# A two-layer kernel whose instruction order is worked out by another model of time

## The chip, the cores and the metric

One core of a Trainium2 chip runs the whole program. A core has five engines with an instruction stream each, which meet only at semaphores: TensorE (PE in the profile, with its weight loads as PEld), VectorE (DVE), ScalarE (ACT), GpSimd (POOL) and SyncE (SP, which here only starts transfers). The metric is the device time of one execution in microseconds. The span of a profile runs from the first to the last instruction of the execution that the profiler recorded.

## The reference, cut to what matters

The input `x` is 4 batches of 512 tokens with 256 features, all in float32. Two layers follow each other.

```
xn = layernorm(x)
x  = x + linear_attention(xn) + gene_ffn(xn)          # layer 0
xn = layernorm(x)
x  = x + gated_mixer(xn) + moe(xn)                    # layer 1
```

- `linear_attention`: q, k, v projections, elu(.)+1 of q and k, the running sum of k times v along the tokens, times q, output projection.
- `gene_ffn`: logits of 512 genes per token, the 32 largest by `top_k`, a softmax over them, their gene vectors, and then tanh of one projection times another.
- `gated_mixer`: q, k, v, running sums of exp(k) v and exp(k) along the tokens, their quotient gated by sigmoid(q), then a SwiGLU block with a hidden width of 1024: `x + u * silu(g) @ w_out.T`.
- `moe`: 16 experts with an inner width of 176, each token goes to its two best, and one shared expert of width 352 sees every token.

## The kernel before, in words

**Stages.** Layer 0 of a batch `b` is `front(b)` (L229: layer norm, transposes, projections, running sum, gene logits) and `back(b, i0, nt)` (L299: for each tile of 128 tokens the top 32 by four rounds of MAX8 and MATCH_REPLACE8 on DVE (L311, L312), then `express` (L321), and at last `out` (L346), the output projection, whose result L352 adds to `xs`). Layer 1 up to the SwiGLU block is `mix(b, i0, nt)` (L366). It takes statistics of `xs` (L203 to L211: DVE, a square root on ACT at L209, DVE), forms `xn` on ACT (L216), transposes it (L224), projects (L389), exponentiates (L415, L416), transposes `qk` and `vs` (L224 again), runs the scans `sums` (L426), two reciprocals of 256 columns for each half of the features (L435), and writes `yT` (L437). It also works out the tokens' two experts (`chosen`, `cwall`). Batch 0's `mix` runs in two halves of 256 tokens, the other batches' in one piece.

**Dense chunks.** The shared expert and the SwiGLU block are one generator, `dense` (L573). It has 8 halves of 256 tokens and 11 chunks of hidden columns in each: three of the shared expert, which need only `xn1T` of their tokens, and eight of the SwiGLU block, which need `yT`. A chunk is 4 matmuls into `gu` (L583; a float32 matmul is two passes in the profile), a nonlinearity into `hid`, and 2 matmuls into `acc` (L606), two chunks behind. The nonlinearity has two forms: while the list `calm` is empty, ACT copies `gu` out and POOL makes three products and sums (L594 to L597); once `calm` holds something, DVE does it in two instructions out of PSUM (L590, L591). Both start with a tanh on ACT (L587). After a half's last chunk L617 adds `acc` to `xs` on DVE.

**Experts.** `route` (L465) counts the tokens of each expert by two matmuls into `pr` (L491, L492) and turns them into row numbers (`slot`, L538). `scatter` (L546) writes the tokens' `xn` to the DRAM array `xrows`, sorted by expert, in 32 indirect transfers that POOL issues (L549). `experts` (L804) goes over 47 tiles of 128 rows in 24 pairs: fetch (`xg`, L741), transposes (L733), up (L770), down (L791), and a store to `yrows` (L802). At the end 32 indirect gathers on POOL (L836) fetch each token's two results as `ys`, and L847 adds them on DVE.

**What sets the order.** The generators are interleaved by hand with `together`, which takes steps from its streams in given proportions; `d(n)` stands for n chunks. That is the order in which instructions are recorded; 66 chunks are recorded before the experts and 22 beside the gathers. The tile framework's scheduler then makes each engine's own order out of the recorded list, by what is ready in its model of time, and gives out semaphores and buffers. `paced` (L92) makes a transfer wait for the last `acc` matmul recorded before it. Each engine runs its instructions strictly in the scheduler's order.

Buffers that matter: PSUM holds 3 `gu` and 1 `acc`, and there are 4 `hid`. `ones` (L107) is the constant row that the scans use, `both` (L593) the copy of `gu` for POOL; its pool `w2` is closed with `mixing` at L703.

Of the kernel before, what the change touches and what calls it, by code (L numbers as in the profile page):

```python
# [11 lines left out]
F32 = mybir.dt.float32  # L12
# [4 lines left out]
P = 128  # L17
B, L, D = 4, 512, 256
NT = L // P
# [11 lines left out]
HB = 2 * P  # L31
# [6 lines left out]
def run_all(steps):  # L38
    for _ in steps:
        pass  # L40


def together(*streams):

    live = [[iter(steps), n, 0] for steps, n in streams]
    while live:
        s = min(live, key=lambda s: s[2] / s[1])
        s[2] += 1
        if next(s[0], live) is live:
            live.remove(s)  # L50
# [3 lines left out]
def tile_two_layers(  # L54
# [21 lines left out]
    out: bass.AP,  # L76
):
    nc = tc.nc
    V, S, G, T = nc.vector, nc.scalar, nc.gpsimd, nc.tensor

    const = ctx.enter_context(tc.tile_pool(name="const", bufs=1))
# [22 lines left out]

    ident = const.tile([P, P], F32, name="ident")
    make_identity(nc, ident)
    ones = const.tile([P, L], F32, name="ones")  # L107
    G.memset(ones, 1.0)

    load_x(0)  # L110
    wqkv = wp.tile([P, NH, 3 * D], F32, name="wqkv")
# [67 lines left out]
    wd = ctx.enter_context(tc.tile_pool(name="wd", bufs=2))  # L179
# [4 lines left out]
    wk = mixing.enter_context(tc.tile_pool(name="wk", bufs=1))  # L184
    w2 = mixing.enter_context(tc.tile_pool(name="w2", bufs=2))
# [3 lines left out]
    def bank():  # L189
        return ps_m.tile([P, L], F32, name="pm")  # L190


    carry = wk.tile([P, 6], F32, name="carry")

# [351 lines left out]
    def scatter():  # L546
        for k in range(2):
            for i in range(NTT):
                sc = G.indirect_dma_start(  # L549
                    out=xrows,  # L550
                    out_offset=bass.IndirectOffsetOnAxis(ap=slot[:, k, i : i + 1], axis=0),
                    in_=xn1[:, i // NT, i % NT],
                    in_offset=None,
                ).ins
                tc.declare_no_dep(sc, group="scatter", reason="no two tokens share a row")
                tc.add_to_no_dep_group("scatter", sc)
                paced(sc)
                yield
# [12 lines left out]
    calm = []  # L571

    def dense():  # L573
# [5 lines left out]
        def up(ins, spare, gw, g0, uw, u0, m, which, dw, dc):  # L579
            gu = ps_d.tile([P, 2, HB], F32, name="gu")  # L580
            for k, (w, at) in enumerate(((gw, g0), (uw, u0))):
                for h in range(NH):
                    T.matmul(  # L583
                        gu[0:m, k], w[:, h, at : at + m], ins[which][:, h], start=(h == 0), stop=(h == NH - 1)
                    )
            th = wd.tile([P, HB], F32, name="th", bufs=2)
            S.activation(th[0:m], gu[0:m, 0], AF.Tanh, scale=0.5)  # L587
            hid = wd.tile([P, HB], F32, name="hid", bufs=4)
            if spare:
                V.scalar_tensor_tensor(th[0:m], th[0:m], 1.0, gu[0:m, 0], ALU.add, ALU.mult)  # L590
                V.tensor_tensor(hid[0:m], gu[0:m, 1], th[0:m], ALU.mult)  # L591
            else:
                both = w2.tile([P, 2, HB], F32, name="both")  # L593
                S.copy(both[0:m], gu[0:m])  # L594
                G.tensor_tensor(hid[0:m], both[0:m, 0], both[0:m, 1], ALU.mult)  # L595
                G.tensor_tensor(th[0:m], th[0:m], hid[0:m], ALU.mult)
                G.tensor_tensor(hid[0:m], hid[0:m], th[0:m], ALU.add)  # L597
            return hid
# [36 lines left out]
    dd = dense()  # L635

    def d(n):
        return islice(dd, n), n
# [29 lines left out]
    m2 = mix(2, 0, NT)  # L668
    next(m2)
    run_all(islice(dd, 2))  # L670
    together((m2, 9), (back(3, 0, NT), 12), d(9))
    first.close()

    weights = ctx.enter_context(ExitStack())
# [7 lines left out]
    def load_experts():  # L682
        wdv = w_down.rearrange("(e i) d -> i e d", i=NI)
        for e in range(0, NE, 4):
            es = slice(e, e + 4)
            for h in range(NH):
                paced(
                    nc.sync.dma_start(
                        wev[:, es, h * 2 * NI : (h + 1) * 2 * NI],
                        w_gate_up[es, h * P : (h + 1) * P, :].rearrange("e p j -> p e j"),  # L690
                    ).ins
                )
                yield
            paced(nc.sync.dma_start(wev[:, es, EW - 2 * D : EW - D], wdv[0:P, es]).ins)
            yield
            paced(nc.sync.dma_start(wev[0 : NI - P, es, EW - D : EW], wdv[P:NI, es]).ins)
            yield

    m3 = mix(3, 0, NT)
    next(m3)  # L700
    run_all(islice(dd, 2))
    together((m3, 9), d(5), (load_experts(), 17))
    mixing.close()  # L703
    routing = ctx.enter_context(ExitStack())
    calm.append(True)
    together((route(), 8), d(5))
    routing.close()
    together((scatter(), 33), d(15))

    run_all(islice(dd, 6))  # L710

    wx = ctx.enter_context(tc.tile_pool(name="wx", bufs=2))
    hbs = []
# [114 lines left out]
    back = ctx.enter_context(tc.tile_pool(name="back", bufs=1, side="right"))  # L828
# [77 lines left out]
```

## Time and profile before

| | us |
|---|---|
| runs | 599.85, 598.52, 599.7; median 599.7 |
| profiled execution | 600.71 |
| its span, first to last instruction | 599.0 |
| PE busy | 544.6 (91%) |
| weight loads busy | 390.5 (65%) |
| DVE busy | 342.2 (57%) |
| ACT busy | 265.9 (44%) |
| POOL busy | 236.2 (39%) |
| DMA queues of SP, and of POOL | 38.53 MB, 8.39 MB |

The busy times of different engines overlap. A stage is bound by the engine that is full in it, or by a chain of waits that goes from engine to engine; which of the two it is can be seen only stage by stage. An instruction's line is that of `kernel.py`; `x8` means that eight of a kind are put together. A wait in brackets is the idle time of the engine just before the instruction, with what ended it. The passes of PE are pipelined: one of 256 columns is listed with 384 ns, while the next one follows after 216 ns.

### The profile page before, as it was taken

To read this page: it belongs to the slowest core of one execution; us is meant where nothing else is said; L and a number is where in the kernel's file an instruction comes from. 1 tells how busy PE (TensorE), PEld (TensorE's weight loads), DVE (VectorE), ACT (ScalarE), POOL (GpSimd) and SP (SyncE) were. 2 spreads that over 40 slices of the span, in tenths; PEclk is the share of its full clock that TensorE was granted. 3 is DMA by queue.
4 is the path that set the end of the run, shared out by engine and by line. 5 is a ranking of instruction groups with operands and counts; after the bars stand their busy time and mean duration, and the time that the engine had idled before them with its cause. 6 is when DMAs were issued, how large, how long until landed. Compare 5 with 4: busy or idle time off the path is not lost.

```text
span 599.0 us, 7343 instructions
## 1 busy us (share of the span) xinstructions
PE 544.6 (91%) x2360; PEld 390.5 (65%) x2360; DVE 342.2 (57%) x890; ACT 265.9 (44%) x568; POOL 236.2 (39%) x298
## 2 busy tenths in 40 slices
PE   3949979899999989999899499699999999999897
PEld 1424457655676555756676388587777777788786
DVE  2899998289683949934842982232222222225553
ACT  3667865955467572668178011113333333321111
POOL 1332058386747172666782027650000000006651
PEclk9998979999999999999999989799999999999989
DMA  5992000000000000000069202223233333114441
GB/s 165 393 382 95 1 1 1 1 1 2 0 1 1 0 2 1 2 0 1 0 183 320 77 6 100 88 89 105 89 106 106 107 106 96 54 63 125 130 122 45
DMA packets 38453, 47.38 MB, mean 79 GB/s; under 512 B 4016, under 2 KB 34960, under 8 KB 38160
## 3 DMA queue, kind: packets, MB, share of 16 engines
q1 hardware_dynamic: 35344, 38.53, 19.8%
q0 software_dynamic: 3072, 8.39, 4.6%
q8 instruction: 19, 0.31, 0.2%
q14 instruction: 18, 0.15, 0.1%
HBM read 28.30 MB, written 18.61 MB: 78 GB/s over the span
## 4 chain that ended last, share of the span: by engine, by line
PE 56%; DVE 25%; ACT 7%; POOL 4%; issue 3%; another core or an unknown queue 2%; DMA 1%; SPq 0%; DVEq 0%; POOLq 0%; ACTq 0%
PE gu L583 16%; PE pu L770 9%; PE acc L606 8%; PE py L791 7%; PE pm L389 5%; DVE rep L312 5%; DVE top L311 4%; PE pt L733 3%; DVE sums L435 3%; PE pm L224 2%; DVE sums L426 2%; PE pm L283 2%; PE pm L334 1%; DVE bs L203 1%
## 5 line engine op out<-in xcount | busy, mean ns | idle before, releaser
L583 PE MATMUL gu<-yT,wugt 128*128 128x256 f32 x512 | 125.9, 384 | 0.0
L583 PEld LDWEIGHTS gu<-yT,wugt 128*128 128x128 f32 x512 | 96.8, 192 | 14.0 <-issue 1.4
L587 ACT ACTIVATE th<-gu 128x256 f32<-128x256 f32 (+1 forms) x88 | 33.5, 383 | 162.3 <-PE gu L583 97.6
L836 POOL DMA_INDIRECT ys<-yrows,slot x32 | 30.7, 961 | 153.4 <-PE acc L606 143.1
L606 PE MATMUL acc<-wot,hid 128*128 128x256 f32 x256 | 69.5, 390 | 13.3 <-DVE hid L591 13.3
L770 PE MATMUL pu<-wex,xgT 128*128 x188 | 63.8, 461 | 0.8 <-ACT xgT L747 0.8
L606 PEld LDWEIGHTS acc<-wot,hid 128*128 128x128 f32 x256 | 48.2, 194 | 21.3 <-DVE hid L591 14.1
L583 PE MATMUL gu<-xn1T,sgu 128*128 128x256 f32 (+1 forms) x192 | 51.1, 404 | 0.1
L590 DVE SCALAR_TENSOR_TENSOR th<-th,gu 128x256 f32<-128x256 f32 (+1 forms) x48 | 20.0, 417 | 53.5 <-ACT th L587 39.4
L779 DVE TENSOR_TENSOR hb<-pu,hb 128x176 f32<-128x176 f32 x47 | 16.1, 342 | 51.0 <-ACT hb L778 51.0
L389 PE MATMUL pm<-w,xn1T 128*128 128x512 f32 (+1 forms) x128 | 44.1, 494 | 0.5 <-ACT xn1T L377 0.5
L791 PE MATMUL py<-wex,hgT 128*128 x188 | 44.5, 379 | 0.0
L583 PEld LDWEIGHTS gu<-xn1T,sgu 128*128 128x128 f32 (+1 forms) x192 | 36.6, 196 | 9.8 <-issue 2.6
L595 POOL TENSOR_TENSOR hid<-both 128x256 f32<-128x256 f32 (+1 forms) x40 | 29.7, 743 | 33.5 <-ACT both L594 33.4
L791 PEld LDWEIGHTS py<-wex,hgT 128*128 128x128 f32 x188 | 35.6, 190 | 8.6 <-issue 0.2
L549 POOL DMA_INDIRECT xrows<-xn,slot x32 | 30.9, 966 | 24.9 <-DVE th L590 10.9
L770 PEld LDWEIGHTS pu<-wex,xgT 128*128 128x128 f32 x188 | 32.0, 190 | 11.0 <-ACT xgT L747 1.0
L389 PEld LDWEIGHTS pm<-w,xn1T 128*128 128x128 f32 x128 | 24.0, 190 | 21.6 <-issue 16.5
L783 DVE COPY hgT<-pt 128x512 f32<-128x512 f32 (+1 forms) x24 | 16.3, 680 | 34.2 <-PE pt L733 34.2
L283 PE MATMUL pm<-wct,xnT 128*128 128x512 f32 x64 | 32.4, 640 | 1.1 <-ACT xnT L242 1.1
L311 DVE MAX8 top<-rep 128x8 f32<-128x512 f32 x48 | 32.7, 682 | 0.3
L312 DVE MATCH_REPLACE8 rep<-top,rep 128x512 f32<-128x512 f32 x48 | 32.3, 674 | 0.0
(170 smaller groups left out, 968.2 us busy)
## 6 DMA issues: line engine op xcount, KB each, us to landing
xrows<-zero SPq DMA_DIRECT2D x1, 6016.0 KB, 22.5
xg<-xrows SPq DMA_DIRECT2D x23, 256.0 KB, 2.7
yrows<-yg SPq DMA_DIRECT2D x23, 256.0 KB, 2.1
wex<-in_w_gate_up_dram SPq DMA_DIRECT2D x8, 704.0 KB, 9.9
xs<-in_x_dram SPq DMA_DIRECT2D x4, 512.0 KB
wugt<-in_wug_dram SPq DMA_DIRECT2D x1, 2048.0 KB
wex<-in_w_down_dram SPq DMA_DIRECT2D x4, 512.0 KB
out_dram<-xs SPq DMA_DIRECT2D x7, 256.0 KB, 2.4
```

Source lines behind the costliest of these rows:

```text
L283: T.matmul(pl, xnT[:, h, i * P : (i + 1) * P], wct[:, h], start=(h == 0), stop=(h == NH - 1))
L311: V.max(tp[:, 8 * r : 8 * r + 8], src)
L312: V.match_replace(rep, tp[:, 8 * r : 8 * r + 8], src, TAKEN)
L389: T.matmul(o[:, 0:n], xnT[:, h, i * P : (i + 1) * P], w1[:, h, at : at + n], start=(h == 0), stop=(h == NH - 1),)
L549: sc = G.indirect_dma_start(out=xrows, out_offset=bass.IndirectOffsetOnAxis(ap=slot[:, k, i : i + 1], axis=0), in_=xn1[:, i // NT, i % NT] ...
L583: T.matmul(gu[0:m, k], w[:, h, at : at + m], ins[which][:, h], start=(h == 0), stop=(h == NH - 1))
L587: S.activation(th[0:m], gu[0:m, 0], AF.Tanh, scale=0.5)
L595: G.tensor_tensor(hid[0:m], both[0:m, 0], both[0:m, 1], ALU.mult)
L606: mm = T.matmul(acc[:, t], hid[0:m, t * P : (t + 1) * P], dw[0:m, dc], start=(n == 0 and t == 0), stop=(n == NC - 1), skip_group_check=True,)
L770: T.matmul(pg[:, 0 : 2 * NI], xT[:, i, h], wex[:, bass.ds(at[i] + h * 2 * NI, 2 * NI)], start=(h == 0), stop=(h == NH - 1),)
L791: mm = T.matmul(py[:, i * D : (i + 1) * D], hT[:, i, h], wex[:, bass.ds(at[i] + EW - (2 - h) * D, D)], start=(h == 0), stop=(h == 1),)
L836: G.indirect_dma_start(out=ys[:, asked], out_offset=None, in_=yrows, in_offset=bass.IndirectOffsetOnAxis(ap=slot[:, k, n : n + 1], axis=0) ...
```

## The change

Five edits:

- `tc.block(schedule_with_timeline_sim=True)`: the scheduler works out each engine's order with another, finer model of time.
- `calm.append(True)` moves from before `route` to after it, so that the chunks beside `route` take the form with ACT and POOL.
- The counts of chunks in four `together` calls: 9 to 8 beside batch 3's `back`, 5 to 4 beside batch 3's `mix`, 15 to 18 beside `scatter`, and 6 to 5 after it.
- `both` is taken from the pool `wd`, which stays open, and no longer from `w2`.
- `ones` is taken from the pool `wk`, and its memset is recorded later.

```diff
     nc = tc.nc
+
+    ctx.enter_context(tc.block(schedule_with_timeline_sim=True))
     V, S, G, T = nc.vector, nc.scalar, nc.gpsimd, nc.tensor
...
-    ones = const.tile([P, L], F32, name="ones")
-    G.memset(ones, 1.0)
...
+    ones = wk.tile([P, L], F32, name="ones")
+    G.memset(ones, 1.0)
...
-                both = w2.tile([P, 2, HB], F32, name="both")
+                both = wd.tile([P, 2, HB], F32, name="both")
...
-    together((m2, 9), (back(3, 0, NT), 12), d(9))
+    together((m2, 9), (back(3, 0, NT), 12), d(8))
...
-    together((m3, 9), d(5), (load_experts(), 17))
+    together((m3, 9), d(4), (load_experts(), 17))
     mixing.close()
     routing = ctx.enter_context(ExitStack())
-    calm.append(True)
     together((route(), 8), d(5))
     routing.close()
-    together((scatter(), 33), d(15))
-
-    run_all(islice(dd, 6))
+    calm.append(True)
+    together((scatter(), 33), d(18))
+
+    run_all(islice(dd, 5))
```

Behind the first edit stands the whole instruction order: on every engine most instructions that can move do move. Lines from L109 on shift by up to two; texts here keep the numbers of the kernel before.

## The prediction

> **What bounds it now.** I read the stretches first, then the waits, the chain, and single instructions in order of time.
>
> Busy time in stretches that I cut at landmarks (first `yT` chunk 91, routing matmul `pr` 345.4, first expert 413.2, last expert 532.8); after the stretch: its length, then busy us (and count) of PE, PEld, DVE, ACT, POOL, the granted clock, DMA:
>
> ```profile
> 0.00:91.00 91.00, 67.17 (x205) 34.54 (x206) 77.86 (x233) 57.78 (x104) 27.10 (x43) 0.94 0.49 170
> 91.00:336.00 245.00, 235.17 (x1047) 160.28 (x1046) 161.54 (x424) 147.21 (x323) 145.12 (x185) 1.00 0.12 36
> 336.00:345.40 9.40, 1.38 (x4) 0.83 (x3) 9.22 (x13) 0.38 (x1) 1.23 (x5) 0.80 0.00 1
> 345.40:413.20 67.80, 62.56 (x272) 53.14 (x271) 27.79 (x73) 8.34 (x22) 31.98 (x35) 0.93 0.23 78
> 413.20:532.80 119.60, 118.64 (x571) 90.55 (x570) 32.96 (x73) 43.50 (x95) 0.00 (x0) 1.00 0.29 93
> 532.80:599.00 66.20, 59.73 (x268) 51.16 (x266) 32.85 (x79) 8.71 (x23) 30.74 (x32) 0.96 0.34 99
> ```
>
> PE sets the end nearly everywhere: idle 24 us before 91, 10 us from there to 336, 8 us while DVE makes the last sums, 5 and 1 around scatter and experts, 6.5 at the end. In the start DVE is the full engine. The dense chunks fill PE under the gathers. The waits of PE name the one large hole in the middle (total, times, longest):
>
> ```profile
> PE acc L606 <- DVE hid L591: 15.5, 3, 8.0
> ```
>
> What fixes the tail, from the instructions in order of time (start, length; in brackets idle time and what ended it):
>
> ```profile
> 537.74 0.98 POOL L836 DMA_INDIRECT ys<-yrows,slot  x1 [135.42 <-PE acc L606]
> ...
> 540.28 0.95 POOL L836 DMA_INDIRECT ys<-yrows,slot  x1 [0.30 <-issue]
> 540.50 0.48 DVE L847 SCALAR_TENSOR_TENSOR xs<-ys,cpair,xs 128x256 f32<-128x256 f32 x1 [2.39 <-DMA ys<-yrows,slot]
> ...
> 541.53 0.94 POOL L836 DMA_INDIRECT ys<-yrows,slot  x1 [0.30 <-issue]
> ...
> 594.82 0.69 DVE L617 TENSOR_TENSOR xs<-acc,xs 128x512 f32<-128x512 f32 x1 [1.29 <-PE acc L606]
> 595.54 0.82 SPq L856 DMA_DIRECT2D out_dram<-xs  x2
> ```
>
> The first gather starts 4.9 us after the last expert matmul (532.73 by 531.70 + 1.03); unhindered gathers come every 1.26 us; 2.8 us later DVE may add. Last, the start, where ACT's order matters:
>
> ```profile
> 11.54 1.07 ACT L242 COPY xnT<-pm 128x512 f32<-128x512 f32 x2 [0.57 <-PE pm L224]
> 16.00 0.59 ACT L287 COPY lg<-pm 128x512 f32<-128x512 f32 x1 [3.38 <-PE pm L283]
> 17.78 0.63 ACT L158 ACTIVATE wot<-wot 128x512 f32<-128x512 f32 x1 [1.19 <-DMA wot<-in_wo_dram]
> ```
>
> **The Trainium skill.** "Trainium Architecture — The Big Picture", Inside one NeuronCore: each engine has its own instruction stream, joined only by semaphores; so a waiting instruction holds all behind it on its engine, as ACT's L158 above shows for 1.19 us. "DMA: Bandwidth & Descriptors", Two DMAs through the same engine are not ordered: a dependent DMA must wait for the first one's semaphore. The trace agrees: the last store of `yrows` is issued at 533.2, lands 3.6 later, and no gather starts before 537.74. "Perfetto Trace Analysis", DMA Instruction — SWDGE: such an instruction's end is that of descriptor writing, not of the data: here 0.95 us against 2.8 to the add. "TensorE: Matmul & The Clock Gate", What's actually happening: an idle PE falls to half clock. Agrees: after 5.24 us idle at 381.5 four `acc` passes take 2.07 instead of 1.03, and the next eight `gu` 3.19 instead of 1.89: 2.3 us.
>
> **The change, part by part.** Its own time is 600.71 for the profiled execution, span 599.0 with 1.7 around it; the median of the runs is 599.7. I sum on the span.
>
> (a) Written edits. Three more chunks take the ACT-POOL form: DVE saves 3 × (0.418 + 0.421) = 2.5 us, POOL gets 3 × (0.746 + 0.726 + 0.779) = 6.8, ACT 3 × 0.584 = 1.8. POOL is 39% busy, ACT 44%, so alone this is worth nothing; without that cover it would be 6.8. Its use would be at 336, where `hid` (L591) stands behind `sums` on DVE. `ones` and `both` only change pools; the memset (0.5 us) is needed 24 us later. The moved counts (9, 5, 15, 6 to 8, 4, 18, 5) still give 66 chunks before the experts and 22 after, as written.
>
> (b) The order. The two built programs, instruction by instruction, are what I go by; durations are those of the trace (a chunk is 8 `gu` and 4 `acc` passes at 0.216 us: 2.59). On PE:
>
> ```
>                                     before      after
> chunks begun/done at pr (L491)      44 / 41.5   63 / 60
>   at the first expert tile (L733)   66 / 64     82 / 79
>   at the last expert matmul         66.5 / 64   88 / 88
> ```
>
> All 22 chunks that lay under the gathers now stand ahead of the experts or among the first ones. So L836, still last on POOL and still waiting for all of `yrows`, has no matmul beside it.
>
> (c) Before `pr`: 19 more `gu` groups × 1.73 + 18.5 `acc` groups × 0.865 = +48.8 us of PE.
>
> (d) Start. On ACT, L158 now stands before the copies of `xnT` (L242), and batch 1's L209 and four L216 before the `lg` copies. L158 can't begin before `wot` lands at 17.78, so the first logits on PE (12.18 before) wait until 18.9; x of batch 1 lands at 19.3, its statistics on DVE take 2.3, the sqrt round trip 0.7, L216 2.0; then `lg`, and the first MAX8 starts at 24.9 instead of 16.6. DVE is full from there to `yT`; 3 us of it (batch 1's statistics) are already done, its order has 4 us more ahead of the first `yT`, so `yT` comes at 90.5 + 8.3 - 3 + 4 = 99.8, or 97 where the first matmuls use only its first half. PE has done as much by then as before (57 against 58 us). +6.5.
>
> (e) Starved boundaries. Chunks now run as soon as they can, so they are used up when a batch ends: chunk 22 needs batch 1's `xn1T`. In the new order nothing stands on PE between the output projection of batch 1's last tile (L349) and the transposes of its `xn` (L224), where three chunks stood; the way round is L352, statistics, sqrt, L216: 6.2 us on DVE (with two top-k steps in it) + 0.7 ACT: 6.5. From the transposes of `qk`, `vs` to the first chunk on `yT`, PE work against DVE work: batch 0's second half 4 against 7 (29 us of cover before): 2; batch 1: 10 + 5 against 11.4 + 11.7, top-k steps among the sums: 9.5, of which 3 idle were there before; batch 2: 9 + 2.6 against 9.0 + 7.7: 5.5. Sum 23.5 - 3, about +20.
>
> (f) Given back before `pr`: the 8.0 hole shrinks to about 4, since its chunks' L590 and L591 now stand between the scans, though still behind two pairs of reciprocals; the extra chunks cover some 3 of the 10 us of idle. -7.
>
> `pr` at 345.4 + 48.8 + 6.5 + 20 - 7 = 414 (413.7).
>
> (g) `pr` to the experts. Before: first scatter 12.0 after `pr`, last one 43.9 later, `xg` fetched 2.5 after that, landing 2.7: 61.2. The scatters' paced waits name chunks up to 58, all done at `pr`, so 31 × 1.267 = 39.3 replaces 43.9: 56.5. PE has only 19 chunks there (50.2), waits 6, and runs slowly for 2 us. First expert 414 + 58.5 = 472.
>
> (h) Experts: 119.6 plus what is left of the chunks (6 × 1.73 + 9 × 0.865 = 18.2), less the one `gu` half in the old stretch: 137. Last expert matmul at 609.
>
> (i) Tail: 4.9 to the first gather, 31 × 1.26 = 39.1, 2.8 to the last add, 0.4, L617 (0.7; DVE's order has it after all 32 adds), and 3.5 from its end to the span's end as now: 51.4. End 661, against 4.2 us after the last matmul before. With the 1 to 1.7 around the span: 662.
>
> SP: the order up to `xrows<-zero` is the same; expert weights landed 80 us ahead of need and have 56 us after `pr` alone. POOL: scatters and gathers are last in both.
>
> **Not seen in this trace**: 32 gathers in a row, unpaced. From below 0.95 each (30 us, no issue gap), from above 1.46 (1.16 + 0.30, seen at 545.7): 45. I take 1.26, which four in a row show. The starvation of (e): from below 0, if other work covers it; from above 35, when each wait adds a slow clock and top-k steps queue longer.
>
> **Rivals.** (1) Exposed gathers and starved boundaries as summed: 662; 0.60. (2) PE never starves: the early chunks fill all the idle of 91 to 336 and the hole: 345.4 + 48.8 + 6.5 - 15 = 386 at `pr`, then the same 248: 634. For it: DVE is only two thirds busy there. Against: the order itself leaves nothing to fill. 0.20. (3) Waits pass on: chunk form on DVE beside m3's sums, a slow PE clock after each: `pr` at 440, 690; 0.16. (4) Not slower: the early chunks turn all of PE's idle into work, so that the tail is paid. It decides where the last expert matmul comes by 599 - 51.4 = 547.6; PE is busy 485 us in the first five stretches, and 58 of chunks come to it (21.5 × 1.73 + 24 × 0.865): 543, which leaves 5 us of idle where the start alone had 24. 0.04; about 598. That the flag changes nothing is excluded: the orders differ.
>
> **Numbers.** 662, the first case (640 to 682). The range must hold eight in ten: from below half of (2) to a part of (3): 634 to 686. 0.2% (1.2 us) is about what can be told from no change: faster 0.03, same 0.01, slower 0.96, all from (4) against the rest.
>
> **What would show it.** Gathers in a row from some 5 us after the last `py`, PE idle for 50 us: (i); last `gu` before the fourth pair or so: (b). First MAX8 near 25 and L158 ahead of L242: (d). PE idle before L224 on `xn` of batch 1 and before `yT` chunks: (e). `pr` near 414: the sum of (c) to (f). I'd be wrong if gathers start before the last `yrows` lands, or if `pr` comes under 390 with PE full.

## The result, and the profile after

The changed kernel takes 694.1 us (median of 4 runs, 692.1 to 694.7) beside 599.8 for the kernel before: a ratio of 1.156, 95% interval 1.152 to 1.160. Its profiled execution has a span of 693.0. The direction and the mechanism of the tail were as predicted, the size was not: 662 was forecast, with 686 as the upper end of the range.

The same stretches as before, cut at the same landmarks (first `yT` chunk, which in the kernel before begins at 91.9, a little after the 91.0 of its cut; about the last `sums`, `pr`, first expert tile, last expert matmul); the columns are those of the prediction's first fence:

```profile
0.00:103.53 103.53, 70.06 (x204) 36.28 (x205) 79.39 (x245) 54.59 (x100) 30.25 (x47) 0.91 0.42 150
103.53:421.00 317.47, 283.44 (x1241) 203.95 (x1240) 173.44 (x445) 153.71 (x342) 145.41 (x189) 0.95 0.09 28
421.00:430.45 9.45, 7.87 (x36) 6.94 (x37) 5.23 (x12) 1.15 (x3) 2.23 (x7) 1.00 0.01 2
430.45:506.24 75.79, 54.84 (x233) 46.13 (x232) 25.34 (x66) 7.18 (x19) 30.94 (x32) 0.84 0.21 70
506.24:644.00 137.76, 135.61 (x649) 105.54 (x647) 38.00 (x85) 46.47 (x103) 0.00 (x0) 1.00 0.26 82
644.00:693.00 49.00, 0.00 (x0) 0.00 (x0) 16.18 (x33) 0.00 (x0) 30.32 (x32) 0.54 0.45 131
```

`pr` comes 85 us later than before (430.45 by 345.43). The stretch from there to the experts has grown from 67.8 to 75.8 although PE has less to do in it (54.8 busy by 62.6). In the last 49 us PE has not one instruction. Of PE's waits, as in the prediction's second fence, three have grown or are new; the last line is that of the kernel before:

```profile
PE pm L226 <- ACT xn L218: 24.9, 3, 12.0
PE acc L608 <- DVE th L592: 17.8, 1, 17.8
PE gu L585 <- DVE yT L439: 9.5, 2, 5.8
PE pm L224 <- ACT xn L216: 16.5, 6, 9.6
```

The wait for `xn` was there before, 9.6 us of it at the very start (12.0 now). New is one of 10.6 us at 210.55, for batch 1's `xn`. No wait for `th` or `yT` of this kind was listed before.

The start, ACT and DVE, answers to the prediction's last fence (the lines are now those of the changed kernel, up to two higher):

```profile
11.23 2.08 ACT L218 ACTIVATE xn<-xs,mv,rs 128x256 f32<-128x256 f32 x4 [1.97 <-DVE mv L213]
18.08 0.63 ACT L158 ACTIVATE wot<-wot 128x512 f32<-128x512 f32 x1 [4.76 <-DMA wot<-in_wo_dram]
18.61 1.06 ACT L244 COPY xnT<-pm 128x512 f32<-128x512 f32 x2
22.93 2.07 ACT L218 ACTIVATE xn<-xs,mv,rs 128x256 f32<-128x256 f32 x4 [0.47 <-DVE mv L213]
27.39 0.59 ACT L289 COPY lg<-pm 128x512 f32<-128x512 f32 x1 [2.39 <-PE pm L285]
10.66 0.17 DVE L153 TENSOR_SCALAR nbqk<-bqkv 128x4 f32<-128x4 f32 x1 [1.64 <-DMA bqkv<-in_bqkv_dram]
10.81 0.20 DVE L212 RECIPROCAL rs<-rs 128x8 f32<-128x8 f32 x1
28.01 0.69 DVE L313 MAX8 top<-lg 128x8 f32<-128x512 f32 x1 [4.84 <-ACT lg L289]
```

L158 does stand ahead of the copies of `xnT` and waits 4.8 us for its transfer. There is also one that I had not listed: L153 waits 1.6 us for `bqkv` ahead of L212, and `xn` starts at 11.23 instead of 8.90. This one costs nothing further on, since the copies stand behind L158 until 18.61 anyway.

The tail is as worked out. Gathers come 1.25 us apart from 3 us after the last expert matmul, and L619 (L617 of before) is behind all 32 adds:

```profile
646.46 0.98 POOL L838 DMA_INDIRECT ys<-yrows,slot  x1 [164.86 <-DMA yrows<-yg]
647.75 0.96 POOL L838 DMA_INDIRECT ys<-yrows,slot  x1 [0.30 <-issue]
...
688.28 0.48 DVE L849 SCALAR_TENSOR_TENSOR xs<-ys,cpair,xs 128x256 f32<-128x256 f32 x1 [0.50 <-issue]
688.80 0.69 DVE L619 TENSOR_TENSOR xs<-acc,xs 128x512 f32<-128x512 f32 x1
```

Where the 94 us of span went: 85.0 to `pr`, 8.0 to the first expert (75.8 by 67.8), 17.5 in the experts with the last chunks among them (137.1 by 119.6 up to the end of the last `py`), and 16.6 given back by a shorter tail (49.7 by 66.2).

### The profile page after: what moved, and what is told of

Read it like the earlier page. It is cut to its first block, busy times and chain, and to the rows that moved or that the text cites. A ratio compares the mean times of both kernels' runs of the same rounds, so it can differ in the third digit from the quotient of the medians.

```text
span 693.0 us, 7321 instructions
## 1 busy us (share of the span) xinstructions
PE 551.8 (80%) x2360; PEld 398.8 (58%) x2360; DVE 337.6 (49%) x884; ACT 263.1 (38%) x567; POOL 239.2 (35%) x307
## 3 DMA queue, kind: packets, MB, share of 16 engines
HBM read 28.30 MB, written 18.61 MB: 68 GB/s over the span
## 4 chain that ended last, share of the span: by engine, by line
PE 56%; DVE 17%; ACT 9%; POOL 7%; issue 4%; another core or an unknown queue 3%; DMA 3%; SPq 0%; POOLq 0%; DVEq 0%; ACTq 0%
PE gu L585 17%; PE acc L608 8%; PE pu L772 8%; PE py L793 6%; PE pm L391 5%; POOL ys L838 4%; PE pt L735 3%; DVE rep L314 3%; DVE top L313 2%; PE pm L285 2%; DVE sums L437 2%; PE pm L257 2%; PE pm L336 2%; DVE sums L428 1%
## 5 line engine op out<-in xcount | busy, mean ns | idle before, releaser
L585 PE MATMUL gu<-yT,wugt 128*128 128x256 f32 x512 | 129.5, 399 | 10.3 <-DVE yT L439 9.5
L585 PEld LDWEIGHTS gu<-yT,wugt 128*128 128x128 f32 x512 | 101.9, 201 | 28.2 <-DVE yT L439 10.3
L608 PE MATMUL acc<-wot,hid 128*128 128x256 f32 x256 | 66.6, 386 | 20.2 <-DVE th L592 17.8
L772 PE MATMUL pu<-wex,xgT 128*128 x188 | 59.9, 459 | 0.0
L597 POOL TENSOR_TENSOR hid<-both 128x256 f32<-128x256 f32 (+1 forms) x43 | 31.7, 739 | 68.3 <-ACT both L596 67.6
L585 PE MATMUL gu<-xn1T,sgu 128*128 128x256 f32 (+1 forms) x192 | 46.7, 379 | 0.0
L391 PE MATMUL pm<-w,xn1T 128*128 128x272 f32 (+1 forms) x128 | 45.4, 495 | 0.9 <-ACT xn1T L379 0.8
L772 PEld LDWEIGHTS pu<-wex,xgT 128*128 128x128 f32 x188 | 33.8, 190 | 14.4
L585 PEld LDWEIGHTS gu<-xn1T,sgu 128*128 128x128 f32 (+1 forms) x192 | 34.3, 181 | 8.4 <-issue 2.4
L781 DVE TENSOR_TENSOR hb<-pu,hb 128x176 f32<-128x176 f32 x47 | 16.0, 341 | 38.9 <-ACT hb L780 38.8
L599 POOL TENSOR_TENSOR hid<-hid,th 128x256 f32<-128x256 f32 (+1 forms) x43 | 32.9, 769 | 1.6
L226 PE MATMUL pm<-ident,xn 128*128 128x128 f32 x64 | 11.9, 335 | 26.2 <-ACT xn L218 24.9
```

The costliest lines, as they stand in the source:

```text
L391: T.matmul(o[:, 0:n], xnT[:, h, i * P : (i + 1) * P], w1[:, h, at : at + n], start=(h == 0), stop=(h == NH - 1),)
L585: T.matmul(gu[0:m, k], w[:, h, at : at + m], ins[which][:, h], start=(h == 0), stop=(h == NH - 1))
L608: mm = T.matmul(acc[:, t], hid[0:m, t * P : (t + 1) * P], dw[0:m, dc], start=(n == 0 and t == 0), stop=(n == NC - 1), skip_group_check=True,)
L772: T.matmul(pg[:, 0 : 2 * NI], xT[:, i, h], wex[:, bass.ds(at[i] + h * 2 * NI, 2 * NI)], start=(h == 0), stop=(h == NH - 1),)
```

## The experiments

Every ratio is to the kernel before in the same comparison. Chunks counted at a landmark are those whose `gu` matmuls have begun. The lines in a fence are numbered as in that run's own kernel. A `NoSync` dependence fixes only the order in which the scheduler places two instructions of one engine. Times and ratios are of all executions of a run, what happens within it is from the one that was profiled. "Old order" below is that of the kernel with the written edits alone.

### The flag or the written edits

`edits_alone` takes out the flag:

```diff
-    ctx.enter_context(tc.block(schedule_with_timeline_sim=True))
```

> The changed kernel without the line that asks for the other order: every written edit stays (three more chunks in the form of ScalarE and GpSimd, the counts, the two tiles' pools). Theory 1 (the edits are worth nothing, the order is everything): 44 to 46 chunks are begun at pr, and the time is 598, between 594 and 602. Theory 2 (the edits have a part in the loss, through three chunks' 6.8 us on GpSimd or the moved counts): 606 or more.

Measured: 589.2, ratio 0.9999 (0.9990 to 1.0008). `flag_alone` puts this one line into the kernel before:

> The kernel before with nothing but the line that asks for the other order. Theory 1: 63 chunks are begun at pr as in the changed kernel, so the time is that of the changed kernel, 690, between 683 and 697. Theory 2 (the edits and the order act together): 30 us or more below the changed kernel, 664 or less.

Measured: 678.2, ratio 1.151 (1.148 to 1.154), 63 chunks begun at `pr`. Both times lie under the ranges in us, because the kernel before takes 589.2 in this comparison and 599.8 in the first; the ratios are those of theory 1 in both cases. So the order is all of the loss and the edits are none of it. The edits' aim can be seen: PE's hole ahead of the last `sums` shrinks from 8.0 to 2.8 us; but `pr` comes at 345.2 as before, since it follows DVE's last `sums` and `yT` (341.8 to 343.8), not PE. In `flag_alone` the hole beside the scatters is missing too, which needed runs of its own (below). Without that hole nothing is lost behind `pr`: from there to the end `flag_alone` takes 243.7 us and `edits_alone` 242.4, and 87.1 of the 88.5 us of span that lie between them are lost ahead of it. The 17 chunks that the new order has done early do not make what comes later any shorter.

### Where the chunks stand

`after_bars` gives TensorE two bars, that is, dependences that keep the chunks recorded after a certain matmul behind it; `after_tailbar` has the second alone:

```diff
-                    T.matmul(
+                    mm = T.matmul(
                         gu[0:m, k], w[:, h, at : at + m], ins[which][:, h], start=(h == 0), stop=(h == NH - 1)
                     )
+                    if bar and k == h == 0:
+                        tc.add_manual_dep(
+                            mm.ins,
+                            bar[-1],
+                            mybir.DependencyInfo(mybir.DependencyClass.NoSync, mybir.DependencyReason.DATA),
+                            reason="this chunk lies behind the bar",
+                        )
...
-        T.matmul(pr[:, NTT * NE : L], allone, flat, start=True, stop=True)
+        bar.append(T.matmul(pr[:, NTT * NE : L], allone, flat, start=True, stop=True).ins.name)
...
     together((experts(), NP2 + 2))
+    bar.append(marks[-1])
```

> The changed kernel with two bars for TensorE's order: a chunk recorded after pr may not be put ahead of pr, and one recorded after the experts may not be put ahead of the last expert matmul. All else is ordered as in the changed kernel. Theory 1 (the loss is the chunks' place: a tail with nothing beside the gathers, scatters with too little beside them): what is left is the start (some 12 us) and a few starved boundaries, so 620, between 610 and 632; gathers end within some 12 us of the last chunk. Theory 2 (the other order is bad throughout, wherever the chunks stand): 650 or more.

Measured: 662.6, ratio 1.125 (1.123 to 1.127): theory 2. The tail is covered again (the last add at 650.3, the end at 660.8), but `pr` comes at 405.3 with only 38 chunks begun. PE waits there for the chain, with no chunk in its way (`stri` gets its memory only when the last `yT` is written, at 402.9):

```profile
391.29 0.66 PE L226 MATMUL pm<-ident,vs 128*128 128x128 f32 x4 [0.36 <-DVE sums L435]
405.30 1.22 PE L493 MATMUL pr<-chosen,stri 128*128 128x256 f32 x2 [13.36 <-POOL stri L475]
```

PE is idle for 102.3 us up to `pr`, against 68.8 in `flag_alone` beside it: chunks taken out of the new order leave some of their time as holes.

> The changed kernel with one bar: the 22 chunks that are recorded after the experts may not be put ahead of the last expert matmul on TensorE. Up to pr nothing changes (63 chunks begun there), 3 chunks are left beside the scatters. Theory 1 (the bare tail and the scatters' chunks are paid for twice): pr at 430 to 433 as before the bar, 56 us to the first expert, 120 for the experts, 62 to 66 behind them: 668 to 676. Theory 2 (the 22 chunks cost the same wherever they stand): the time of the changed kernel, within 6 us.

Measured: 673.3, ratio 1.122 (1.118 to 1.126): by the time, theory 1. `pr` at 430.6, 55.6 us to the first expert (PE busy for 11.7 of them), 61.9 behind the last expert matmul. Holding back 22 chunks that the new order had done early is worth some 20 us against `after_again` (693.6, of another comparison, below). But 17.4 of these lie between `pr` and the first expert (55.6 by 73.0), where `after_again` has the hole and this run, with three chunks left there, has none. In `flag_alone`, without the hole, the same stretch takes 55.6 us with all its chunks. What the experts gain (123.5 by 137.1) the tail loses nearly whole (61.9 by 49.7). So the double payment of theory 1 is not shown: most of the gain is that of the hole.

`pe_recorded` makes each chunk's first matmul follow the TensorE instruction recorded just before it (`told` lists their names):

```diff
+                    if k == h == 0:
+                        tc.add_manual_dep(
+                            mm.ins,
+                            told[-2],
+                            mybir.DependencyInfo(mybir.DependencyClass.NoSync, mybir.DependencyReason.DATA),
+                            reason="a chunk stays behind what was recorded before it",
+                        )
```

> The changed kernel, but on TensorE no chunk may be put ahead of a TensorE instruction that the program records before it; the other engines' orders are left to the same model of time. 38 chunks are begun at pr, 64 at the first expert tile, 22 lie behind the experts. Theory 1 (chunks put ahead of the chain's own matmuls are what delays pr): pr at 370 or earlier where the two bars gave 405, the time 620 to 630. Theory 2 (VectorE's and ScalarE's own orders delay it): pr at 390 or later, the time 645 to 662.

Measured: 651.4, ratio 1.082 (1.080 to 1.085); `pr` at 390.5 with 38 chunks begun. By the bounds set, theory 2: with no chunk in the chain's way, `pr` is still 45 us late, with six chunks less done than in the kernel before. Which engine's order it is, this run can't tell: the rest of TensorE's order is the model's too.

### The hole beside the scatters

In the changed kernel PE stops for 17.8 us in the middle of the scatters. The timelines of ACT, PE and POOL there:

```profile
461.04 0.38 ACT L589 ACTIVATE th<-gu 128x256 f32<-128x256 f32 x1 [8.06 <-PE gu L585]
484.15 0.39 ACT L589 ACTIVATE th<-gu 128x256 f32<-128x256 f32 x1 [22.73 <-remote]
486.38 0.66 ACT L589 ACTIVATE th<-gu 128x256 f32<-128x256 f32 x2 [1.84 <-remote]
458.08 1.89 PE L585 MATMUL gu<-yT,wugt 128*128 128x256 f32 x8
467.34 0.38 PE L585 MATMUL gu<-yT,wugt 128*128 128x256 f32 x1 [0.73 <-issue]
485.50 2.07 PE L608 MATMUL acc<-wot,hid 128*128 128x256 f32 x4 [17.79 <-DVE th L592]
480.64 0.96 POOL L551 DMA_INDIRECT xrows<-xn,slot  x1 [0.30 <-issue]
```

The `gu` passes that start at 458.08 are over by 460.0, and those of the chunk ahead of them by 457.4; ACT, idle, takes the latter up at 484.15, 26.8 us late, and the former at 486.38. The last scatter's issue ends at 481.6. Up to 449 each tanh in this stretch followed its last `gu` pass by 0.04 us at most; the next ones were 0.4, 6.3 and then 26.8 us late. A tanh waits for PE's semaphore and for DVE's. DVE's is not late: the product that ends at 462.34 is followed by PE at 462.39. Nor is ACT's: the tanh that ends at 461.42 is followed by DVE at 461.46. PE's shows 461.0 and then nothing up to 484.1. That record alone would be weak, since it also lacks updates of ACT on which DVE acted at once; but with the others ruled out, what is late is PE's update, or the completion that raises it. I call this the hold. The kernel before shows the same at 380, where a pause of POOL ends it, and where the record has five updates of PE between 380.11 and 380.41, for passes that were over by 376.3:

```profile
376.63 0.96 POOL L549 DMA_INDIRECT xrows<-xn,slot  x1 [0.30 <-issue]
380.43 0.95 POOL L549 DMA_INDIRECT xrows<-xn,slot  x1 [2.84 <-remote]
380.13 0.66 ACT L587 ACTIVATE th<-gu 128x256 f32<-128x256 f32 x2 [9.48 <-remote]
```

My reading: there POOL's next scatter waited for a chunk's `acc` whose update was itself held up, the queue ran empty, and the updates came through. In the changed kernel the scatters' waits name chunks that are long done, so nothing interrupts them.

`before_nopace` takes the paced wait out of the kernel before; the order of instructions stays as it was:

```diff
                 tc.add_to_no_dep_group("scatter", sc)
-                paced(sc)
```

> The kernel before without the dependence that makes each scatter wait for a chunk's last matmul; all instructions stay in the same order. Theory 1 (pauses let held semaphore updates of TensorE through): where a chip holds them, a hole of some 20 us opens ahead of acc beside the scatters and the time is 10 to 18 us longer; where it does not, 32 scatters take 39.3 us from first to last and nothing else changes, the time within 3 us. Theory 2 (pauses have no part in it): the same holes as in the kernel before of the same chip.

`after_again` is the changed kernel itself, in the same comparison:

> The changed kernel again, beside the others of this comparison. Theory 1 (the hole of 17.8 us beside the scatters comes from this chip or execution, not from the order): no such hole, pr to the first expert 56 us instead of 75.8, ratio to before as for the order alone, 1.147 to 1.156. Theory 2 (the hole belongs to the order): it is there again, with 70 us or more from pr to the first expert.

Measured: `after_again` 693.6, ratio 1.152 (1.149 to 1.155), theory 2, with a hole of 17.1 and 73.0 us from `pr` to the first expert. `before_nopace` 615.2, ratio 1.023 (1.020 to 1.025), theory 1: 32 scatters in 39.7 us, and then

```profile
374.29 0.38 ACT L586 ACTIVATE th<-gu 128x256 f32<-128x256 f32 x1 [5.75 <-PE gu L582]
389.01 0.38 ACT L586 ACTIVATE th<-gu 128x256 f32<-128x256 f32 x1 [14.34 <-remote]
401.69 0.66 ACT L586 ACTIVATE th<-gu 128x256 f32<-128x256 f32 x2 [12.29 <-remote]
```

with holes of 10.8, 1.7, 2.4 and 3.0 us on PE; the first expert comes at 429.9 instead of 413.2. So an unbroken run of scatters is what lengthens the hold, and the waits that looked like mere pacing were worth 13 us here. `pe_recorded`, in the same comparison, agrees from the other side: its scatters pause seven times, by 0.5 to 2.2 us, and no tanh beside them is over 1 us late. So do the other runs with the hold: the longer the longest unbroken run of scatters, the later the latest tanh.

| longest unbroken run | latest tanh, us late | runs |
|---|---|---|
| 8 | 0.9, 0.8 | `pe_recorded`, `rec_VT_start` |
| 16 | 9.1 | `before` |
| 21 | 14.4, 17.3 | `taken_T`, `taken_VT` |
| 23, 24 | 17.0 to 18.0 | `edits_again`, `taken_VST`, `taken_VT_wot`, `taken_V` |
| 28 | 24.5 | `taken_S` |
| 32 | 25.8 to 28.8 | `before_nopace`, `after_again`, changed kernel, `after_start` |

A hold that sets in some 11 us after the first scatter and lasts to the end of the run would give about these figures: 16, 23 and 32 scatters at 1.267 us, less 11, are 9.3, 18.1 and 29.5 us (an estimate). One update did come through at 389.0 without a pause: the hold is not strict.

It is not always there. In the comparison with `flag_alone` there is no hold at all; the tanhs go on at the chunk's pace through 32 unbroken scatters, and `pr` to the first expert takes 55.6 us:

```profile
469.62 0.38 ACT L589 ACTIVATE th<-gu 128x256 f32<-128x256 f32 x1 [2.21 <-PE gu L585]
472.21 0.38 ACT L589 ACTIVATE th<-gu 128x256 f32<-128x256 f32 x1 [2.21 <-PE gu L585]
474.80 0.38 ACT L589 ACTIVATE th<-gu 128x256 f32<-128x256 f32 x1 [2.21 <-PE gu L585]
```

The kernel before took 589.2 there and 599.4 to 601.7 in all the others. Each comparison ran on one chip of its own, so whether it is the chip or the occasion can't be told. `after_drain8`, in that comparison, was to make pauses by a dependence of every eighth scatter on the one before it:

```diff
+                done.append(sc.name)
+                if len(done) % 8 == 1 and len(done) > 1:
+                    tc.add_manual_dep(
+                        sc,
+                        done[-2],
+                        mybir.DependencyInfo(mybir.DependencyClass.Sync, mybir.DependencyReason.DATA),
+                        reason="the scatters so far have landed",
+                    )
```

> The changed kernel, but every eighth scatter also waits until the scatters before it have landed: three pauses, of some 2.5 us each. Theory 1 (TensorE's semaphore updates are held back while indirect DMAs follow each other without a pause, and come through in a pause): the hole of 17.8 us ahead of acc shrinks to under 6, the last scatter starts some 7 us later, the first expert some 12 us earlier, and the time is 682, between 677 and 687. Theory 2 (the hole has another cause, in TensorE's order or its instructions): the hole stays, and the time is 694 to 702.

Measured: 676.8, ratio 1.148 (1.146 to 1.151), with no pause (the longest pitch is 1.47 us) and no hole to remove: it decides nothing. `edits_again` is `edits_alone` in a comparison with the hold:

> The written edits without the other order, again, beside the others of this comparison. If TensorE's updates are held back beside the scatters (a chip as in the first comparison), theory 1: three more chunks beside the scatters in the form of VectorE change nothing, 598 to 602; theory 2: scatters that wait for other chunks pause less and the time is 5 us or more above the kernel before. If they are not held back: the time of the kernel before within 2 us.

Measured: 602.6, ratio 1.0035 (1.0014 to 1.0055), with `acc` held for 4.9 and 7.6 us beside the scatters. Neither theory's bound is met exactly; the edits are worth nothing in the one comparison and cost 2.5 us in the other (interval 0.8 to 3.3).

### First tries at the start and at VectorE's order

`after_start` moves the start's instructions back: L158 behind the first copy of `lg`, L153 and L155 behind batch 0's scales, batch 1's statistics and square root behind batch 0's first top-k step and its exp.

```diff
-    S.mul(wot, wot, QSCALE)
...
     run_all(islice(f0, 4))
+    behind_of(V.tensor_scalar(nbqk, bqkv[:, 0:4], -1.0, None, ALU.mult), ("sl", 0))
+    behind_of(V.tensor_scalar(bqkv1, bqkv[:, 0:4], 1.0, None, ALU.add), ("sl", 0))
+    behind_of(S.mul(wot, wot, QSCALE), ("lg", 0, 0))
```

> The changed kernel with its start put in the order of need: ScalarE scales wot (L158) after the first copy of lg, VectorE does L153 and L155 after batch 0's scales, and batch 1's statistics and square root stand behind batch 0's first top-k step and its exp. The rest is ordered as in the changed kernel. Theory 1 (the late start passes on to the end): the first MAX8 starts near 17 instead of 28, the first chunk on yT near 93 instead of 103.5, pr 10 us earlier, the time 8 to 12 us shorter. Theory 2 (what comes later waits for something else anyway): pr moves by under 3 us, and so does the time.

Measured: 702.2, ratio 1.167 (1.164 to 1.170). The first MAX8 came at 21.6 instead of 28, and the first chunk on `yT` at 105.7: no earlier. My dependences had pushed batch 1's statistics behind batch 0's top-k, while TensorE's order still had batch 1's transposes ahead of the second half of batch 0's output projection, which then waited 10.0 us for them. It shows a mend that made a new wait, and neither theory.

`rec_V_start` and `rec_VT_start` hold VectorE, and then TensorE too, to the recorded order, by a NoSync dependence of each instruction on the one of its engine recorded before it; the weights' instructions are moved as above, with the scalings of `wot1` and `sdn` too.

```diff
+                if self.last is not None:
+                    tc.add_manual_dep(
+                        r.ins,
+                        self.last,
+                        mybir.DependencyInfo(mybir.DependencyClass.NoSync, mybir.DependencyReason.DATA),
+                        reason="the order as recorded",
+                    )
+                self.last = r.ins.name
```

> The changed kernel, but VectorE keeps the order in which the program records its instructions, and the weights' own instructions (wot, wot1, sdn on ScalarE; L153 and L155 on VectorE) stand behind batch 0's logits. TensorE, the rest of ScalarE and GpSimd are ordered by the model of time as in the changed kernel; TensorE's order follows by itself: 46 chunks begun at pr, 65 at the first expert tile, 19 behind the last expert matmul. Theory 1 (VectorE's order, the start included, is what delays the chain that leads to pr): first MAX8 near 17, first chunk on yT at 92 to 97, pr at 350 to 368, the time 600 to 628. Theory 2 (ScalarE's or TensorE's order delays it): pr at 380 or later, the time 640 or more.

> As the one before, and TensorE too keeps the recorded order (38 chunks begun at pr, 66 at the first expert tile, 22 behind the experts); only ScalarE and GpSimd are left to the model. Theory 1 (between them the two orders explain the loss): pr at 340 to 362, the time 598 to 622. Theory 2 (ScalarE's and GpSimd's orders hold a part of their own): pr at 375 or later, 635 or more.

Measured: 712.9, ratio 1.184 (1.177 to 1.190), and 702.3, ratio 1.169 (1.166 to 1.172); `pr` at 455.5 and 441.0. Both are worse than the changed kernel. I had taken the recorded order for the old one; it is not, the old scheduler reorders too. By their bounds these runs would speak for theory 2, but they tested the wrong order and say nothing on the new one.

### One engine's old order at a time

What could be taken over is the old order itself. At the end of the program each kept engine's instructions (`kept.all`, as recorded) are chained in the places that they have in the kernel with the edits alone. `taken_T` keeps TensorE's, `taken_V` VectorE's, `taken_S` ScalarE's, the others several; `taken_VT_wot` adds the same kind of dependence from the scaling of `wot` to batch 0's first copy of `lg`:

```diff
+    for kept, places in ((T, PLACES_T),):
+        for one, other in zip(places, places[1:]):
+            tc.add_manual_dep(
+                kept.all[other],
+                kept.all[one].name,
+                mybir.DependencyInfo(mybir.DependencyClass.NoSync, mybir.DependencyReason.DATA),
+                reason="the order of the kernel with the edits alone",
+            )
```

> The changed kernel, but TensorE is held, instruction by instruction, to the order that it has in the kernel with the edits alone (46 chunks begun at pr, 66 at the first expert tile, 22 behind the experts); VectorE, ScalarE, GpSimd and SyncE stay with the model of time. Theory 1 (TensorE's order is the cause): pr at 345 to 362, the time 600 to 620. Theory 2 (VectorE's order is): pr at 380 or later, 635 or more, since the chain still runs through its order. Theory 3 (ScalarE's order is, by what stands ahead of the copies that feed TensorE): as theory 2 here.

> The changed kernel, but VectorE is held to the order that it has in the kernel with the edits alone; the others stay with the model of time, which then begins 48 chunks ahead of pr, 66 ahead of the first expert tile, and leaves 19 behind the last expert matmul. Theory 1 (TensorE's order): 650 or more. Theory 2 (VectorE's order): pr at 350 to 370, the time 605 to 630. Theory 3 (ScalarE's order): pr at 380 or later, 635 or more.

> The changed kernel, but ScalarE is held to the order that it has in the kernel with the edits alone; the others stay with the model of time, which then begins 49 chunks ahead of pr, 69 ahead of the first expert tile, and leaves 19 behind the last expert matmul. Theory 1 and theory 2: pr at 380 or later, 640 or more. Theory 3 (ScalarE's order): pr at 350 to 370, the time 605 to 630.

> The changed kernel with TensorE and VectorE both held to the orders of the kernel with the edits alone; ScalarE and GpSimd stay with the model. Theories 1 and 2: all but a few us of the loss is gone, 598 to 612. Theory 3: the loss up to pr stays, 635 or more.

> TensorE and VectorE held to the orders of the kernel with the edits alone, and one instruction of ScalarE moved: the scaling of wot stands behind the first copy of lg instead of ahead of the copies of xnT. The rest of ScalarE's order and GpSimd's are the model's. Theory 1 (with the two engines held, this one instruction is what is left of the delay of pr): the first MAX8 near 17, the first chunk on yT near 92, pr at 345 to 350, the time 600 to 608. Theory 2 (it is worth its own wait of 7 us and no more, the rest is spread over ScalarE's order): pr at 352 to 355, the time 608 to 612.

> TensorE, VectorE and ScalarE all held to the orders of the kernel with the edits alone; only GpSimd and SyncE are left to the model of time. Theory 1 (GpSimd's and SyncE's orders cost nothing): pr at 344 to 347, the time that of the edits alone, 599 to 605. Theory 2: 607 or more.

Each theory of a single engine fails at its own run: `pr` comes at 381.7 in `taken_T`, 421.1 in `taken_V` and 405.3 in `taken_S`. `taken_VT` falls between the bounds, and `taken_VST` is on the side of its theory 2.

As a ladder, from all old to all new. The rows come from four comparisons, all of them with the hold. PE idle up to `pr` is `pr` less PE's busy time up to there:

| new orders | label | us | ratio (95%) | `pr` | chunks begun | PE idle to `pr` |
|---|---|---|---|---|---|---|
| none | `edits_again` | 602.6 | 1.0035 (1.001–1.006) | 345.1 | 46 | 34.3 |
| GpSimd, SyncE (and whatever else the flag sets) | `taken_VST` | 608.6 | 1.016 (1.012–1.021) | 351.2 | 46 | 42.0 |
| + ScalarE, but for one instruction | `taken_VT_wot` | 613.1 | 1.024 (1.019–1.029) | 356.7 | 46 | 45.3 |
| + ScalarE | `taken_VT` | 617.6 | 1.028 (1.024–1.032) | 360.5 | 46 | 49.6 |
| + VectorE | `taken_T` | 641.7 | 1.071 (1.067–1.075) | 381.7 | 46 | 68.6 |
| + TensorE (the changed kernel) | `after_again` | 693.6 | 1.152 (1.149–1.155) | 431.9 | 63 | 69.1 |

The rows behind the last two steps (time up to `pr`, then busy PE, PEld, DVE, ACT, POOL, clock, DMA), first of `taken_VT`, then `taken_T`, then `after_again`:

```profile
0.00:360.49 360.49, 310.93 (x1278) 201.97 (x1278) 248.37 (x666) 208.41 (x433) 178.97 (x243) 0.97 0.21 68
0.00:381.72 381.72, 313.15 (x1279) 204.34 (x1279) 250.30 (x666) 206.00 (x431) 178.94 (x243) 0.95 0.19 64
0.00:431.94 431.94, 362.87 (x1481) 248.17 (x1481) 258.17 (x700) 209.38 (x445) 177.92 (x243) 0.94 0.17 56
```

TensorE's new order adds 49.7 us of work ahead of `pr` (362.87 less 313.15; 17 `gu` groups × 1.73 + 16.5 `acc` groups × 0.865 is 43.7, the rest I put down to slower passes) and, on balance, half a us of idle time. VectorE's order adds 19 us of idle time and 2 of busy time. ScalarE's adds 7.6, GpSimd's and SyncE's together 7.7. No single theory of the three holds: in this sequence TensorE's order is the largest part, and most of the added idle time comes with the other engines' orders.

Three things limit these prices. Executions with the same order differ: the kernel before has 41.7 us of PE idle up to `pr` and `before_nopace` 39.3. The profiled execution of `taken_VT` was 2.6 us above its median and that of `taken_T` 2.8 below, so that VectorE's step is rather larger than the table has it (24 us of median time). And the ladder was climbed in one sequence only. The balance for TensorE hides two changes, as the stretches up to the first `yT` chunk and from there to `pr` show (of `taken_VT`, then `taken_T`):

```profile
0.00:102.74 102.74, 68.27 (x211) 35.80 (x211) 76.97 (x233) 58.36 (x105) 28.43 (x45) 0.92 0.45 151
102.74:360.50 257.76, 242.67 (x1071) 166.18 (x1069) 171.41 (x433) 150.05 (x329) 150.55 (x199) 0.99 0.12 34
0.00:110.04 110.04, 71.51 (x210) 36.84 (x211) 84.46 (x256) 59.64 (x107) 28.95 (x46) 0.88 0.40 141
110.04:381.72 271.68, 241.65 (x1071) 167.50 (x1069) 165.84 (x411) 146.36 (x325) 149.99 (x198) 0.98 0.11 33
```

PE is idle for 34.5 and 15.1 us in `taken_VT`, 38.5 and 30.0 in `taken_T`, and 33.5 and 35.6 in the changed kernel. TensorE's new order takes 5 us of holes from the start and adds 5.6 after it.

The scaling of `wot`, one instruction, is worth 3.8 us of `pr` (360.5 to 356.7), hardly more than the executions differ by, and the intervals of the two ratios overlap; the first logits come 7.4 us earlier (19.81 to 12.40), and more than half of that is lost again by the first chunk on `yT` (99.8 by 102.7). Neither bound was met, theory 2 is the nearer.

Taken over alone, VectorE's old order gives 679.7 (ratio 1.135, 1.129 to 1.140) and ScalarE's 664.7 (1.109, 1.105 to 1.113). The model then also begins fewer chunks ahead of `pr` (48 and 49) and leaves 19 for the tail, so these two mix an engine's own order with what it changes on TensorE; they are no shares. PE's idle time up to `pr` is 89.6 and 72.6 us in them, more than in the changed kernel: one engine's old order among new ones can do harm.

## Why the prediction was wrong

**(a) Right.** 0.9999 and 1.0035: the edits cost between nothing and 2.5 us.

**(b) and (c) right.** 63 chunks begun at `pr`, 82 at the first expert tile, 88 at the last expert matmul, as the order said. The extra work of 48.8 us shows in PE's busy time up to `pr`:

```profile
0.00:345.43 345.43, 303.74 (x1254) 195.65 (x1255) 248.66 (x667) 205.37 (x428) 173.48 (x232) 0.98 0.22 71
0.00:430.45 430.45, 361.37 (x1480) 247.17 (x1481) 258.06 (x700) 209.45 (x445) 177.89 (x243) 0.94 0.17 57
```

It grew by 57.6: 48.8, and 8.8 of slower passes that I had put at nothing (the granted clock up to there fell from 0.98 to 0.94).

**(d), (e), (f): the first step that failed.** "+6.5", "+20" and "-7" made 19.5 us; measured are 27.4 us more idle time (69.1 by 41.7) and those 8.8 of slow passes, 36.2 in all. Up to the first `yT` chunk PE idles 33.5 us instead of 23.8, so (d) is 9.7 for 6.5. From there to `pr` it idles 35.6 instead of 17.9, so (e) and (f) together are 17.7 for 13.

(d): MAX8 came at 28.0 and not 24.9, and `yT` chunks from 103.5 and not 97. I had taken `lg` to be ready when ACT ends batch 1's `xn`, as it does at 25.0. The first `lg` copy then waits until 27.39 for PE, whose new order puts six passes of a projection between the passes of the first logits:

```profile
19.23 3.78 PE L285 MATMUL pm<-wct,xnT 128*128 128x512 f32 x4 [5.18 <-ACT xnT L244]
22.81 2.83 PE L257 MATMUL gu<-xnT,wqkv 128*128 128x512 f32 x6
25.47 2.74 PE L285 MATMUL pm<-wct,xnT 128*128 128x512 f32 x6
```

With TensorE's old order, in `taken_T`, the first MAX8 comes at 24.0.

(e): the waits that I named are there for the most part, but not at their sizes: 10.6 for 6.5 at batch 1's `xn`, and at `yT` none for 2, 3.8 for 9.5 and 5.8 for 5.5. That they make 20.1 for 23.5 in sum is luck. The cause that I gave, that chunks "are used up when a batch ends", is at most a part of it. With the chunks in their old places `taken_T` has 30.0 us of idle time in that stretch, of which VectorE's new order brings 15 (`taken_VT` has 15.1); the new places of the chunks come with 5.6 more. What I took for a shortage of chunks is, in this sequence, for the larger part a chain that VectorE's new order makes later. (f) was right at its one place: the hole of 8.0 at the last `sums` is 2.1.

**(g): the second step that failed.** 58.5 us was predicted from `pr` to the first expert, "waits 6" among them; 75.8 were measured, with PE idle for 21.0 of them, and 55.6 in the comparison without the hold. The wait of 5.24 us at 381.5 was in front of me, and the tanh that led to it had waited 9.48 us for something "remote". I took it as a fixed cost to carry over. It was a cost that grows with the scatters' unbroken run, and my own statement that their waits were all met took its limit away.

**(h) and (i) right.** 137 us for the experts (137.1), and 51.4 for the tail (49.7): 31 gathers took 38.8 us for 39.1 forecast, and the first came 3.1 us after the last expert matmul instead of 4.9. The 4.9 of the kernel before held a wait for an `acc` matmul, as the bracket of its first gather says; here that bracket names the last store of `yrows`.

The sum: 16.7 us missing at `pr` and 17.3 at (g), less 1.7 at (i), are the 32 us between 661 and 693.

**The rivals.** (3) had 690 and `pr` at 440 by waits that pass on, which is the nearest in time; `pr` came at 430 and the rest was the hold, so it is half right. (2) is refuted by PE's idle time. (4) put its limit at a last expert matmul by 547.6; it ended at 643.3.

**Left open**: which instructions of VectorE's order make the 19 us; what the engines' orders would cost if they were taken over in another sequence; why PE's updates alone are held, and only in some comparisons; and whether pauses made for the purpose would gain more than they cost.

## What to carry to other kernels

Work pulled ahead of a chain costs the chain its full length wherever the engine was already full, and does not come back where it used to cover a transfer that takes its time anyway: count it at both places. An order worked out by a model must be judged engine by engine. Taking over the old orders step by step gives each a price, which no single mend of a visible wait did; but it is a price in that sequence, among those neighbours. A wait that looks like mere pacing may be what bounds a contention, so when a change makes such waits moot, look for what they had kept short.

## What the hardware showed that was not expected

Beside back-to-back indirect scatters (0.96 us each, 0.30 between) TensorE's semaphore updates arrive late in four of the five comparisons on record and in the first result: on time for the first 11 us of the run, then up to 26.8 us late in the changed kernel. They come through after a pause (377.6 to 380.13) or when the scatters end; there the first came 2.5 us after the last issue in the changed kernel (481.6 to 484.15) and 0.4 in `after_again`. How late they get goes with the length of the unbroken run: at most 1 us with 8 scatters in a row (`pe_recorded`), 9.1 with 16, 26.8 with 32. ScalarE's and VectorE's updates in the same stretch are on time wherever a reader shows it (0.04 and 0.05 us at 461.4 and 462.3). "Trainium Architecture — The Big Picture", Inside one NeuronCore, in the Trainium skill says that engines synchronize only through semaphores; this case adds that an engine whose work is done can still be, for its readers, 27 us behind. The kernel before takes 599.4 to 601.7 us in the comparisons with the hold and 589.2 in the one without.
